# A two-layer graph network with residual and LayerNorm: splitting x from two buffers, zeroing only outer columns of the counts, four permits for counting, last two groups swapped

## The chip, the cores and the metric
One core of a Trainium2 chip runs the kernel. The metric is device microseconds of one execution. TensorE is called PE in the profile, VectorE DVE, ScalarE ACT, GpSimd POOL, SyncE SP.

## What is computed
The graph has N = 6250 nodes with D = 256 features and E = 100000 edges, sorted by destination; low nodes have the most edges. The reference is

```python
def agg(h, eps):                       # src, dst: (E,)
    return (1.0 + eps) * h + segment_sum(h[src], dst, N)
h = agg(x, eps1)                       # N x 256
h = relu(h @ W1a + b1a)                # 256 -> 512
h = relu(h @ W1b + b1b)                # 512 -> 512
h = agg(h, eps2)                       # N x 512
h = relu(h @ W2a + b2a)                # 512 -> 512
out = layernorm(x + h @ W2b + b2b)     # 512 -> 256, then over the features
```

## The kernel before
Nodes lie in NT = 49 tiles of 128 rows (the last has 106), edges in 782 chunks of 128. There are two ways to sum over edges.

**Light nodes: gathers.** For nodes above the first ten tiles (first eight in layer 2), GpSimd gathers the 128 source rows of a chunk with an indirect DMA (`gather`, L496), four chunks to a piece, six pieces of buffer. TensorE sums them with a matrix that selects slots (`sums`, L1180, L1211). Chunks form 78 groups, of which layer 1 takes the last 75 from the top down (`order`). `merge` (L1230) splits each sum in two parts on ScalarE and VectorE, moves it to node rows with two more matmuls (L1256) and adds it to the accumulators `acc` (L1268). When all groups that reach a tile are in, `dense` (L1289) runs the two matrix products of the layer on a block of one or two tiles (L1334, L1383, L1412) and stores the rows. The `acc` of layer 1 start as rows of x (`seeding`), scaled on ScalarE (`scaling`, L1081).

**Heavy nodes: counts.** For the ten lowest tiles, a matrix of edge counts from source to destination is built and multiplied with all of x. The 340 lowest chunks are counted in 245 steps, from high to low: 31 steps of one chunk in a window of W = 11 destination columns (two banks each), 149 steps of one chunk and width 7 to 10, 65 steps of two to eight chunks. A step (`counting`, L1851) makes two one-hot matrices on VectorE (`ca` L1883, `cb` L1893), multiplies them (L1936) into a bank, and then `counted_` (L1957) copies w - 1 columns of the window from the bank into the counts `at` or `at_first` with ScalarE (L1977) and adds the window's top column there with VectorE (L1985); the place comes from a register. So each copy overwrites columns and the top column is added to what the step before it wrote. Before, both count buffers are zeroed whole on ScalarE (`zeroing`, L1900; eight copies), and no step writes until that is done. A step takes a permit (`permits`, SIDE = 3) and returns it after its add; one-chunk steps of width 10 or less ask for two permits together:

```python
n = max(2 // (STEPS[i][1] * len(parts_of(STEPS[i][2]))), 1)
for _ in some:
    held_.append((yield ("get", permits, 0)))
```

In layer 1, `first_products` (L1668) multiplies the counts with x in three passes (tiles 9 and 8, then 7 to 4, then 3 to 0; L1811). A pass starts when the steps down to its lowest tile are done. For pass 0, `splitting` (L1677) loads four tiles of x into one buffer `raw`, cuts two tiles at a time into an upper and a lower part (two ScalarE copies L1696 and L1697, one VectorE subtraction L1699), and `storing` writes them to `halves` in HBM; `loading` reads them back for passes 1 and 2 once the last store is done. The count matrices are saved to HBM as well (L1783). In layer 2, `second_products` (L1528) multiplies them with h1 in 13 ranges of four tiles (the last, range 12, has one tile), from range 12 down to 0: counts are cast on ScalarE (`converting`, L1575), multiplied (L1648), and each product is added to `acc` (`taking`, L1586 and L1591). The rows of the first SOONER = 2 ranges are loaded and halved before layer 1 ends (`sooner`, L1762).

**Order of the work.** Preparation (up to the branch) turns the edge lists, builds tables and compares the data with the kernel's assumed bounds on VectorE (`violated`, L721); the sum of the violations is reduced at L834 and decides between `ordered` (this kernel) and a slow `general` branch. In `ordered` no engine order is dynamic: while the program is built, a class `Plan` (L296) plays all processes with estimated costs; engines, banks and buffers go to the process with the lowest number first, and the order in which it grants them is the order of each engine's instructions. Counting and sums ask for TensorE with 0, products of layer 1 with 1, dense work with 2, products of layer 2 with 3; SyncE's loads are issued where the plan reaches them. Each engine then runs its list in order and waits where a real time is later than the planned one. `filling` (L1275) puts dummy matmuls (L1280) into planned gaps late in layer 1 and at the start and in the second half of layer 2.

## Time and profile before

| | |
|---|---|
| median of 3 runs | 1537.58 us (1535.27 to 1547.84) |
| the profiled execution | 1526.32 us, of which the span is 1524.6 us |
| PE (matmul) busy | 1297.8 us, 85% of the span |
| DVE, ACT, POOL busy | 811.6 us (53%), 618.4 us (41%), 895.2 us (59%) |
| granted TensorE clock, mean | 0.935 |
| DMA | 304.29 MB, 200 GB/s in the mean |

The profile belongs to one execution; a row gives a line of the kernel, an engine, an operation, and what it writes and reads. An idle time is charged to the instruction after it and to what released that instruction; "issue" means that the view shows nothing it waited for, "remote" that it waited for something the view does not name. A granted clock of 0.50 is 1.2 GHz, 1.00 is 2.4 GHz.

### The profile page before, as it was taken

The numbers are of one execution on the slowest core, as the hardware profiler recorded it, in microseconds if no ns is written. First come the engines' busy times: TensorE is split into PE (matmuls) and PEld (weight loads), VectorE is DVE, ScalarE is ACT, GpSimd is POOL, SyncE is SP. The second block draws the span as 40 slices with busy tenths as digits, with TensorE's granted clock in tenths as the row PEclk, the third lists the DMA queues.
The fourth block names the chain that finished last, engine by engine and source line by source line (L and its number), as shares of the span: only waits on it lengthen the run. The fifth ranks groups of instructions, "written<-read, shape, count | busy, mean of one in ns | idle before, by whom it ended". The sixth has DMA issues, their size and how long they took to land.

```text
span 1524.6 us, 20531 instructions
## 1 busy us (share of the span) xinstructions
PE 1297.8 (85%) x6367; PEld 820.3 (54%) x6367; DVE 811.6 (53%) x2122; ACT 618.4 (41%) x1293; POOL 895.2 (59%) x944
## 2 busy tenths in 40 slices
PE   3478978879888899889968999997989999979997
PEld 2135545436554445555545666665556665656665
DVE  5575756655567883113146665764455544534343
ACT  3656556545555434444533423323233323321211
POOL 7565665565666766661256656664666666656640
PEclk7589988989999999999989999999999999999999
DMA  4555666647774436893478767776677877767650
GB/s 122 163 168 177 221 210 201 204 126 228 235 229 127 119 117 197 272 288 106 160 253 303 228 199 255 225 217 213 210 238 245 259 235 234 221 178 210 199 163 27
DMA packets 154445, 304.29 MB, mean 200 GB/s; under 512 B 34606, under 2 KB 69254, under 8 KB 154328
## 3 DMA queue, kind: packets, MB, share of 16 engines
q0 software_dynamic: 59136, 182.25, 39.6%
q1 hardware_dynamic: 87716, 107.04, 21.6%
q10 hardware_dynamic: 7476, 13.60, 2.5%
q8 instruction: 54, 0.88, 0.2%
q14 instruction: 63, 0.52, 0.1%
HBM read 263.18 MB, written 39.63 MB: 199 GB/s over the span
## 4 chain that ended last, share of the span: by engine, by line
PE 69%; DVE 9%; issue 8%; another core or an unknown queue 4%; ACT 4%; DMA 2%; POOL 1%; DVEq 1%; ACTq 1%; SPq 0%; POOLq 0%
PE bank L1383 17%; PE bank L1412 15%; PE bank L1211 11%; PE bank L1648 9%; PE bank L1811 7%; PE bank L1936 4%; PE bank L1256 4%; PE bank L1334 2%; DVE at L1985 1%; DVE cb L1893 1%; DVE acc L1591 1%; DVE acc L1268 1%; DMA xh<-halves 1%; DVE sel L1160 1%
## 5 line engine op out<-in xcount | busy, mean ns | idle before, releaser
L504 POOL DMA_INDIRECT early<-in_x_dram,srcs x442 | 435.9, 986 | 256.4 <-issue 113.0
L504 POOL DMA_INDIRECT early<-h,srcs x238 | 229.7, 965 | 186.5 <-issue 61.5
L504 POOL DMA_INDIRECT late<-h,srcs x236 | 227.2, 963 | 139.8 <-issue 59.1
L1268 DVE SCALAR_TENSOR_TENSOR acc<-bank,mask,acc 128x512 f32<-128x512 f32 (+1 forms) x365 | 210.9, 611 | 80.0 <-PE bank L1256 21.4
L1383 PE MATMUL bank<-zt,wide_w 128*128 128x256 f32 (+2 forms) x832 | 191.4, 387 | 24.5 <-ACT zt L1355 15.3
L1412 PE MATMUL bank<-wide_w,ht 128*128 128x512 f32 (+1 forms) x392 | 188.5, 607 | 3.2 <-DVE xh L1699 3.2
L1383 PEld LDWEIGHTS bank<-zt,wide_w 128*128 128x128 f32 x832 | 159.6, 203 | 55.6 <-ACT zt L1355 17.4
L1211 PE MATMUL bank<-early,sel 128*32 128x256 f32 (+1 forms) x1360 | 157.4, 489 | 30.2 <-issue 20.3
L1648 PE MATMUL bank<-upper,cfs 128*128 128x512 f32 (+1 forms) x392 | 169.4, 432 | 14.6 <-issue 10.9
L1811 PE MATMUL bank<-cf,xh 128*128 128x512 f32 (+2 forms) x588 | 150.2, 389 | 17.1 <-ACT cf L1752 10.2
L1648 PE MATMUL bank<-xr,cfs 128*128 128x512 f32 (+1 forms) x392 | 155.5, 397 | 0.0
L1977 ACT CAST at<-bank 128x250 f32 (+4 forms) x238 | 113.9, 494 | 99.7 <-PE bank L1936 32.6
L1575 ACT CAST cfs<-ci 128x512 fp32r<-128x512 uint8 (+3 forms) x104 | 60.7, 595 | 220.8 <-PE bank L1648 80.1
L1936 PE MATMUL bank<-cb,ca 128*128 128x490 f16 (+7 forms) x371 | 96.2, 340 | 58.6 <-DVE cb L1893 20.0
L1591 DVE TENSOR_TENSOR acc<-bank,acc 128x512 f32<-128x512 f32 x96 | 65.3, 684 | 137.9 <-remote 50.0
L1160 DVE TENSOR_TENSOR sel<-iota,slot 128x256 f32<-128x256 f32 (+3 forms) x109 | 47.6, 436 | 164.8 <-PE bank L1211 122.2
L1811 PEld LDWEIGHTS bank<-cf,xh 128*128 128x128 f32 (+1 forms) x588 | 100.8, 196 | 50.5 <-issue 20.7
L1256 PE MATMUL bank<-split,to 128*128 128x512 f32 (+3 forms) x306 | 89.8, 398 | 38.7 <-DVE split L1246 19.4
L1893 DVE TENSOR_SCALAR cb<-numbers,spot 128x492 f16<-128x492 f16 (+7 forms) x340 | 99.8, 330 | 40.0 <-remote 12.1
L1383 PE MATMUL bank<-zt,narrow_w 128*128 128x256 f32 (+2 forms) x432 | 103.3, 387 | 6.5 <-issue 4.0
L1211 PEld LDWEIGHTS bank<-early,sel 128*32 128x32 f32 x1360 | 40.0, 112 | 127.0 <-issue 107.0
L1412 PEld LDWEIGHTS bank<-wide_w,ht 128*128 128x128 f32 (+1 forms) x392 | 71.2, 193 | 66.7 <-issue 59.6
(150 smaller groups left out, 1702.4 us busy)
## 6 DMA issues: line engine op xcount, KB each, us to landing
xh<-halves SPq DMA_DIRECT2D x48, 512.0 KB
halves<-xh SPq DMA_DIRECT2D x24, 512.0 KB
h<-h1r ACTq DMA_DIRECT2D x48, 256.0 KB
xr<-h SPq DMA_DIRECT2D x12, 1024.0 KB
acc<-h SPq DMA_DIRECT2D x18, 512.0 KB
early<-in_x_dram,srcs POOLq DMA_INDIRECT x442
raw<-in_x_dram SPq DMA_DIRECT2D x12, 512.0 KB
r<-in_x_dram SPq DMA_DIRECT2D x22, 256.0 KB
```

The source lines that it names most:

```text
L504: nc.gpsimd.indirect_dma_start(out=rows_[:, j, :], out_offset=None, in_=table, in_offset=bass.IndirectOffsetOnAxis(ap=srcs[:, c : c + 1], ...
L1211: mm = nc.tensor.matmul(pm[b * SLOTS : (b + 1) * SLOTS], sel[:, c - groups[g][0], :], rows_[:, l, :], start=(c == part[0]), stop=(c == par ...
L1256: nc.tensor.matmul(pu[:, i * width : (i + 1) * width], to[:used], split[:used, l, i * width : (i + 1) * width], start=(l == 0), stop=(l == 1),
L1268: nc.vector.scalar_tensor_tensor(acc[t], pu[:, i * width : (i + 1) * width], mask[:, t - lo[g], g : g + 1], acc[t], op0=ALU.mult, op1=ALU.add,
L1383: nc.tensor.matmul(ph[:, (f - o) * TILES * P : (f - o) * TILES * P + nb], wa[:, k, f * P : (f + 1) * P], zt[:, k, :nb], start=(k == 0), st ...
L1412: nc.tensor.matmul(po[:m], ht[:, f, i * P : i * P + m], wb[:, f, :], start=(f == 0), stop=(f == KH - 1),)
L1591: nc.vector.tensor_tensor(acc[t], bank[token.number][:, :width], acc[t], op=ALU.add)
L1648: nc.tensor.matmul(bank[token.number][:, :width], cf[:m, j, :], of[:m, j, :], start=(j == 0 and of is upper), stop=(j == len(ks) - 1 and o ...
L1811: nc.tensor.matmul(to[:, :c], of, factor, start=(k == 0 and l == 0), stop=last, skip_group_check=True,)
L1893: made = nc.vector.tensor_scalar(token.tile[:, :e], numbers[:, :e], spot[:, c : c + 1], None, op0=ALU.is_equal,)
L1936: mm = nc.tensor.matmul(bank[token[l].number][:, : (k1 - k0) * w], a.tile[:, c % BATCH, :], b.tile[:, k0 * w : k1 * w], start=(j == 0), st ...
L1977: nc.scalar.copy(of[:, k0:k1, UNDER - w + 1 :][:, :, bass.ds(v, w - 1)], ap[:, :, : w - 1],)
```

## The change
- SIDE, the number of counting permits, goes from 3 to 4.
- `zeroing` writes, instead of all of `at`, only the columns from 976 on and those below 72 of its 1188, and all of `at_first`: three copies instead of eight. As the columns between are no longer zero, a step's top column must lie in the window that the step above it wrote. Preparation compares this for every step (`apart`), from a copy of the step's last nodes in SBUF (`before_`, ScalarE); the old compare of window widths stays for the first eight columns only.
- `splitting` has RAWS = 2 buffers of two tiles each; the planned wait before it goes from 60 to 50 (SPLIT), loads are issued as buffers come free, and a buffer is released once both ScalarE copies have read it. The scratch of the numbering moves to a tile of `ht_room`.
- In layer 1 the last two groups (4, then 3) change places. ENDING becomes a pair, 4 for layer 1 and 3 for layer 2.
- Layer 2 takes its ranges in the order 11, 10, ..., 0, 12, and `sooner` prepares ranges 11 and 10.

```diff
-SIDE = 3
+SIDE = 4
+SPLIT = 50.0
+RAWS = 2
-ENDING = 3
+ENDING = (4, 3)
+LAST = 0
...
+    def turn_order(number):
+        down = list(reversed(range(BEGIN[number - 1], NG)))
+        ending, down = down[:LAST], down[LAST:]
+        if number == 1:
+            down[-2:] = reversed(down[-2:])
+        return down + ending[::-1]
...
+        before_ = prep.tile([P, NC], F32, name="before_")
+        nc.scalar.copy(before_, cp)
         for k in range(halves):
             nc.scalar.copy(src_f[k], src_raw[k])
...
-        violated(compare, NC, near, wide_of, op=ALU.is_ge)
+        violated(compare, taken[0][2], near[:, : taken[0][2]], wide_of[:, : taken[0][2]], op=ALU.is_ge)
...
+        def apart(v):
+            for a, b, n, w in taken:
+                if a:
+                    add_compare(
+                        v[:, a - least_n : a - least_n + n], cp[:, a : a + n], -float(w),
+                        before_[:, a - 1 : a].to_broadcast([P, n]), op0=ALU.add, op1=ALU.is_ge,
+                    )
+                if b - a > n:
+                    add_compare(
+                        v[:, a + n - least_n : b - least_n], cp[:, a + n : b], -float(w),
+                        before_[:, a : b - n], op0=ALU.add, op1=ALU.is_ge,
+                    )
...
         violated(behind, NC - least_n)
+        violated(apart, NC - least_n)
...
+        range_order = [*reversed(range(len(ranges) - 1)), len(ranges) - 1]
...
-                raw_room = Tiles(loan, [P, RANGE, width], F32, "raw", 1)
-                scratch = raw_room.take()
+                raw_room = Tiles(loan, [P, PAIR, width], F32, "raw", RAWS)
+                scratch = ht_room.take()
...
-                rs = list(reversed(range(len(ranges))))
+                rs = range_order
...
                 def splitting():
-                    yield ("rest", 60.0)
-                    for r, ks in enumerate(ranges):
+                    yield ("rest", SPLIT)
+                    landed = []
+                    for q, ks in enumerate(spans):
                         raw = yield ("get", raw_room, 0)
                         in_rows(ks, raw.tile, table)
-                        yield ("rest", LOAD)
...
+                        landed.append(Event(plan))
+                        plan.at(plan.now + LOAD, landed[q].set)
+                        plan.start(parting(q, ks, raw, landed))
+
+                def parting(q, ks, raw, landed):
+                    yield ("until", landed[q])
+                    if q:
+                        yield ("until", parted[q - 1])
...
+                    nc.scalar.copy(xh[:m, :n, 0, :], of)
+                    nc.scalar.copy(ap, of)
+                    raw.release()
+                    parted[q].set()
...
-                    for i, r in enumerate(reversed(range(len(ranges) - SOONER, len(ranges)))):
+                    for i, r in enumerate(range_order[:SOONER]):
...
                 def zeroing():
-                    for k, (of, i, n) in enumerate(
-                        [(at, i, 7) for i in range(0, NT, 7)] + [(at_first, 0, NT)]
-                    ):
-                        some = of[:, i : i + n, :].rearrange("p a b -> p (a b)")
+                    over = (LOW[STEPS[0][0]] - BASE + UNDER) // 4 * 4
+                    under = -(-(HIGH[FINE] - BASE + UNDER + 1) // 4) * 4
+                    for some in (at[:, :, over:], at[:, :, :under], at_first):
                         some = some.bitcast(F32)
...
+                        nc.scalar.copy(
+                            some, zero.unsqueeze(2).to_broadcast(list(some.shape))
+                        )
```

## Rows read from the trace of the kernel before
**Rows 1.** The page, its first line.
```profile
span 1524.6 us, 20531 instructions
```
**Rows 2.** Windows by stage: stretch, length, busy time and count by engine, clock, DMA.
```profile
28.40:60.00 31.60, 10.31 (x52) 4.50 (x53) 15.78 (x49) 22.16 (x23) 21.50 (x22) 0.50 0.65 200
60.00:280.00 220.00, 176.62 (x897) 99.72 (x896) 145.99 (x403) 129.35 (x290) 132.34 (x136) 0.87 0.60 188
280.00:320.00 40.00, 26.53 (x124) 14.71 (x121) 25.74 (x71) 18.99 (x39) 19.93 (x22) 0.82 0.54 168
320.00:460.00 140.00, 124.22 (x631) 76.17 (x630) 79.66 (x224) 76.89 (x157) 88.07 (x91) 0.97 0.71 214
460.00:580.00 120.00, 105.21 (x534) 53.61 (x533) 94.97 (x308) 50.79 (x109) 79.77 (x79) 0.99 0.40 119
580.00:700.00 120.00, 109.13 (x543) 66.62 (x542) 25.71 (x55) 51.74 (x140) 76.48 (x80) 0.99 0.80 248
700.00:745.00 45.00, 44.66 (x206) 25.57 (x204) 11.44 (x21) 15.21 (x40) 0.00 (x0) 1.00 0.24 89
745.00:800.00 55.00, 38.99 (x155) 25.00 (x156) 18.79 (x33) 25.69 (x50) 31.96 (x33) 0.88 0.74 248
```
**Rows 3.** Timeline of VectorE in preparation: start, length, instruction, idle time before.
```profile
12.66 0.15 DVE L759 TENSOR_TENSOR viol<-cp,dstf 128x4 f16<-128x4 f32 x1
...
16.22 0.97 DVE L803 SCALAR_TENSOR_TENSOR viol<-heads,dstf 128x176 f16<-128x176 f32 x6
...
26.87 0.64 DVE L834 TENSOR_REDUCE fsum<-fp 1x1 f32<-1x473 f32 x1 [7.57 <-remote]
```
**Rows 4.** Timeline of TensorE and ScalarE, 40 to 60 us.
```profile
41.25 0.72 ACT L1081 ACTIVATE acc<-acc,e 128x512 f32<-128x512 f32 x1 [8.82 <-issue]
...
44.08 1.08 PE L1936 MATMUL bank<-cb,ca 128*128 128x275 f16 x4 [13.26 <-DVE cb L1893]
...
58.62 1.90 ACT L1977 CAST at<-bank 128x250 f32 x6
```
**Rows 5.** Groups on ScalarE, 40 to 60 us: busy, mean ns, idle before.
```profile
L1912 ACT COPY at<-zero 128x2079 f32<-128x2079 f32 x5 | 9.6, 1914 | 0.0
...
L1912 ACT COPY at_first<-zero 128x3381 f32<-128x3381 f32 x1 | 3.0, 3014 | 0.0
```
**Rows 6.** Groups on TensorE, 80 to 580 us, and on GpSimd, 60 to 580 us.
```profile
L1936 PE MATMUL bank<-cb,ca 128*128 128x490 f16 (+7 forms) x339 | 86.8, 333 | 39.0 <-issue 11.8 <-DVE cb L1893 6.8 <-DVE at L1985 6.4
...
L504 POOL DMA_INDIRECT early<-in_x_dram,srcs x325 | 320.8, 987 | 200.3 <-issue 82.3 <-PE bank L1211 45.8 <-PE bank L1936 41.4
```
**Rows 7.** Windows of the copy out of the bank (L1977, into at) alone.
```profile
80.00:120.00 40.00, 12.33 (x35) 0.83 0.53 170
...
200.00:240.00 40.00, 8.00 (x14) 0.88 0.65 205
...
560.00:600.00 40.00, 2.17 (x6) 1.00 0.53 155
```
**Rows 8.** The tile raw: ns min/median/max, first and last start in us.
```profile
L1696 ACT CAST xh<-raw x25: 395/619/641, 89.9 to 292.5; 128x512 fp32r<-128x512 f32 x24, 106x256 fp32r<-106x256 f32 x1
...
L867 SPq DMA_DIRECT2D raw<-in_x_dram x14: 338/373/535, 78.1 to 277.9; - x14
```
**Rows 9.** Timeline of TensorE and ScalarE at the change of layers.
```profile
746.24 0.50 PE L1648 MATMUL bank<-upper,cfs 106*128 106x512 f32 x1 [1.51 <-ACT cfs L1575]
...
753.44 0.40 PE L1648 MATMUL bank<-xr,cfs 106*128 106x512 f32 x1
...
754.37 0.39 PE L1648 MATMUL bank<-upper,cfs 128*128 128x512 f32 x1
754.60 0.39 PE L1648 MATMUL bank<-xr,cfs 128*128 128x512 f32 x1
...
775.33 0.62 ACT L1575 CAST cfs<-ci 128x512 fp32r<-128x512 uint8 x1 [12.04 <-remote]
...
776.00 0.80 PE L1648 MATMUL bank<-upper,cfs 128*128 128x512 f32 x1 [10.32 <-issue]
```

More of the change, by code (lines that the diff above doesn't have):

```diff
@@ L482, in tile_gin_residual_layernorm @@
         ]
+    def turn_order(number):
[4 more added lines that the diff above has]
+        return down + ending[::-1]
+    turns_of = {number: turn_order(number) for number in (1, 2)}
     pieces = {
@@ L486, in tile_gin_residual_layernorm @@
             (g, members[g][i : i + BURST])
-            for g in reversed(range(BEGIN[number - 1], NG)) for i in range(0, len(members[g]), BURST)
+            for g in turns_of[number] for i in range(0, len(members[g]), BURST)
         ]
@@ L939, in layer @@
             once = number == 1
-            order = list(reversed(range(BEGIN[number - 1], NG)))
+            order = turns_of[number]
             kk = width // P
@@ L983, in layer @@
             for t in reversed(range(NT)):
-                single = last_use.get(t, -1) >= len(order) - ENDING
+                single = last_use.get(t, -1) >= len(order) - ENDING[number - 1]
                 if taken and not single and len(taken) < TILES and (t >= tiles or (tiles - 1 - t) % TILES):
@@ L1145, in selecting @@
             def selecting():
-                for g in order:
+                for at_, g in enumerate(order):
                     if g in sels:
@@ L1150, in selecting @@
                     gs = [g]
-                    if h == 1 and g > order[-1] and groups[g - 1][1] == 1 and len(members[g - 1]) == PARTS:
+                    if (
+                        h == 1 and order[at_ + 1 : at_ + 2] == [g - 1] and groups[g - 1][1] == 1
+                        and len(members[g - 1]) == PARTS
+                    ):
                         gs.insert(0, g - 1)
@@ L1569, in converting @@
                 def converting(r, t, n, token, a):
-                    i = (len(ranges) - 1 - r) * tiles + t
+                    i = rs.index(r) * tiles + t
                     yield ("rest", LOAD)
@@ L1674, in first_products @@
                 stored = [Event(plan) for _ in spans]
+                parted = [Event(plan) for _ in spans]
                 factors = {}
                 def splitting():
[L1678 to L1679 removed]
+                    yield ("rest", SPLIT)
+                    landed = []
+                    for q, ks in enumerate(spans):
                         raw = yield ("get", raw_room, 0)
                         in_rows(ks, raw.tile, table)
[L1682 to L1706 removed]
@@ new lines, in splitting @@
+                        landed.append(Event(plan))
[5 more added lines that the diff above has]
+                        yield ("until", parted[q - 1])
+                    m, n = rows(ks[0]), len(ks)
+                    token = yield ("get", xh_room, 0)
+                    token.users = 2
+                    xh = token.tile
+                    of = raw.tile[:m, :n, :]
+                    bank_ = yield ("get", banks, 1)
+                    yield ("on", "ACT", 2 * act(n * width), 1)
+                    ap = bank[bank_.number][:m, : n * width].rearrange(
+                        "p (k d) -> p k d", d=width
+                    )
[3 more added lines that the diff above has]
+                    parted[q].set()
+                    yield ("on", "DVE", dve(n * width), 1)
+                    nc.vector.tensor_tensor(
+                        xh[:m, :n, 1, :], ap, xh[:m, :n, 0, :], op=ALU.subtract
+                    )
+                    bank_.release()
+                    xh_of[0, q] = token
+                    plan.then(halved[0, q].set)
+                    plan.then(plan.start, storing(q, token))
```

34 lines of the change are left out of this document (3 added, 31 removed).

## The prediction
> **What bounds the kernel now.** Read the page's span first [rows 1]: 1524.6 us, in an execution that took 1526.3 us, 11.3 us under the median of 1537.6 us of the runs shown. Then the windows by stage [rows 2], each of which has another limit. Preparation and the first stage of layer 1, up to 60 us, have TensorE at work for a third of the time or less: 10.3 of 31.6 us between 28.4 and 60, and at a granted clock of 0.50, the lower of its two levels (1.2 GHz). From 60 to 580 us TensorE works 80 to 89% of each stage, and no other engine does more; its idle time there adds up to 43.4 + 13.5 + 15.8 + 14.8 = 87.5 us. From 580 to 700 us it is at 91% with the DMA share at 0.80, from 700 to 745 us it is full (44.7 of 45). At the change of layers, 745 to 800 us, it loses 55.0 - 39.0 = 16.0 us. Behind that the change moves little. So the work of TensorE is fixed, and the question for each edit is which of its gaps closes.
>
> Three views say what makes those gaps. In the first stage, the timeline [rows 4] shows the first counting matmuls on TensorE at 44.08 us, but the first copy out of their banks on ScalarE only at 58.62 us. In between ScalarE works almost without a pause, and most of it is zeroing: of the seven copies into at, 1.914 us each, five lie there, and the one of 3.014 us into at_first [rows 5]. In the middle, the groups [rows 6] charge 39.0 us of TensorE's idle time between 80 and 580 us to the counting matmul (L1936), the largest share of any line, and GpSimd waits 41.4 us for that same line before it may start its next gathers. The rate of counting [rows 7] falls from 35 copies in 40 us to 14 after the one-chunk steps of width 10 and less begin, and counting ends only in the window 560 to 600; the last pass of products cannot start before. The splitting of x [rows 8] runs from 89.9 to 292.5 us, 25 pieces, 8.1 us each where the cast of a piece takes 0.62 us; the reloads for the later passes wait for its last store.
>
> **The change part by part.**
> *Preparation, +1 us.* The diff adds 32 compare instructions on VectorE. Nearest rows: a narrow compare takes 0.15 us, six compares of 176 columns take 0.97 us, so 0.16 us each [rows 3]. 32 x 0.16 = 5.2 us is the upper end. Behind them VectorE stands still for 7.57 us, until 26.87 us, before the reduction that decides the branch. No row names what it waits for. If that is an event of its own, the cost is 0; if it follows VectorE, 5.2. I take 1, near the lower end, because 7.57 covers 5.2. The added copy to before_ stands ahead of the conversion of the sources on ScalarE's queue and waits for the matmul of cp, so the sources and the gathers behind them come later too; that delay lies in the same 7.57. Were that cover gone, the sum would get 5.2 instead of 1. One further compare shrinks from 340 columns to 8, and one matmul is added: nothing, in the same cover.
>
> *Zeroing, -9 us.* The two rows of [rows 5] give (3014 - 1914) / (3381 - 2079) = 0.845 ns a column and 157 ns fixed. The three new copies have 49 x 53 = 2597, 49 x 18 = 882 and 3381 columns: 2.35 + 0.90 + 3.01 = 6.3 us against 16.4. They fit before 41.25 us, where ScalarE now stands idle for 8.82 us ahead of its first scaling [rows 4]; so what goes from the path is all zeroing after 41.25: five copies of 1.914 and the one of 3.014, 12.6 us. Next in line are the scalings between them and the splits of the first sums, which TensorE and GpSimd wait for as well, so gathers and counting both move forward. Bounds: 0 (the rows of acc land late and hold ScalarE anyway) and -12.6. I take -9, nearer the end that the continuous occupation of ScalarE supports.
>
> *Four permits instead of three, -6 us.* A step holds a permit from before its matmuls until VectorE has added its top column. The 149 one-chunk steps of width 10 and less ask for two permits at a time, so three permits let one pair run and four let two. Between 200 and 240 us there were 14 copies, that is 7 pairs, 5.7 us a pair, while ScalarE and VectorE work about 60% of that time [rows 2, 7]: the pairs wait for each other, not for an engine. Counting should end well before 560, and the last products with it. But TensorE had other work meanwhile; only its gaps count. Bounds: a third of the 87.5 us of idle time, -29, and +41.4, if more counting ahead of the sums doubles GpSimd's wait at that line. I take -6, less than a sixth of the 39.0 us charged to L1936, since TensorE is already near 85%.
>
> *Splitting from two buffers, begun 10 planned us earlier, -2 us.* The first load is issued at 78.1 and its rows are cast from 89.9 on [rows 8]: 11.8 us in which, with one buffer, no piece is ready. With two the load of one lies under the casts of the other. What is gained is a share of the 13.5 us that TensorE loses between 280 and 320, where pass 0 ends and pass 1 has no reloaded rows yet. Bounds 0 and -13.5; I take -2, because the counts of pass 1 are needed as well. The 12 further loads of SyncE's queue cost about 0.37 us each there [rows 8], 4.5 us over 200 us, ahead of halves stores and later seeds, which have time. The Trainium skill, DMA: Bandwidth & Descriptors, section "Anatomy of one DMA", gives each transfer a fixed cost of about 2.0 us, which speaks against two loads where there was one: an estimate of 24 us on the chain of loads, and if none of it overlapped this term would be 0 and the sum -21. No row here separates that fixed part.
>
> *Scratch of the numbering in ht's tile, selecting along the new order, ENDING (4, 3):* nothing. The last use of each tile gives the same blocks, and the first ht is wanted long after the numbering.
>
> *Last two groups of layer 1 swapped, 0.* Tile 8 is complete one group sooner. TensorE is full from 700 to 745 [rows 2], so the order of its last work shifts no end. Bounds +-2.
>
> *Ranges 11 and 10 ahead of layer 2 instead of 12 and 11, -7 us.* Range 12 has one tile: its 16 products stretch from 746.24 to 753.84 us [rows 9], 7.6 us, because each pair waits for a cast of its own on ScalarE. A matmul here follows the one before it after 0.23 us, so 16 are 3.7 us: 4 us of TensorE are lost, and with four-tile ranges a cast of 0.62 us serves eight matmuls. Then TensorE stands for 10.32 us until 776.00, behind ScalarE, which waits 12.04 us until 775.33 for something that the view does not name. With 64 products of range 10 at hand I count 3 of these 10 as filled. Bounds 0 and -16.0, the whole idle time of the window. The three more tiles to halve ahead (six copies of 512 columns, by the cast's 0.62 us some 3.7 us of ScalarE) lie in 700 to 745, where ScalarE works 15 of 45 us. Range 12 comes last now, with the same products as before.
>
> Sum: 1 - 9 - 6 - 2 + 0 - 7 = -23 us; 1526.3 becomes 1503, and the median 1537.6 becomes **1515 us**.
>
> **The rivals.**
> *Given back later (0.27), about 1532.* Layer 1 ends when the last sums and their dense work do, and TensorE is full there. If the gathers' chain gains nothing (it waits 45.8 us for the sums at L1211 and 41.4 at L1936 [rows 6], an order that the plan sets anew), the head start turns into more waiting before 580, and only the change of layers and a little of the start stay: -7 + 1 = -6. For it: 580 to 745 is nearly full. Against it: the gathers wait for TensorE, and TensorE's first sums wait for ScalarE.
> *Counting crowds out the sums (0.13), about 1561: slower.* Place: L1936 on TensorE's queue, ahead of L1211. With two pairs in flight GpSimd's 41.4 us behind L1936 double; +41.4 less the other terms (-9 - 2 - 7 + 1 = -17) is +24. It decides once the added wait passes 17 us. For it: the 31 steps of width 11 hold two banks each, and four of them hold all eight. Against it: banks come free earlier too, and 6.4 and 6.8 us of L1936's idle time are waits for the step before [rows 6].
> *The middle closes (0.12), about 1492.* Counting ends 80 us sooner, the last pass spreads over 460 to 580, where the DMA share is 0.40, and a third of the 87.5 us goes: -29 - 9 - 7 + 0 = -45.
> *The stricter compare sends the kernel down its general branch (under 0.01).* From the reference's destination list, every step's last node leaves at least two columns to the step below; the branch stays.
>
> **How the numbers follow.** The forecast has 0.48 and, with its terms' bounds, its own range 1500 to 1527. The range over the cases reaches from just below the closed middle (1490) to 1545, where some of the crowded case is left out. A measurement of this kernel can tell about 1%, 15 us, from no change. Faster by more: 0.8 of the forecast's 0.48, and the closed middle's 0.12: 0.50. Within: the rest of the forecast and nearly all that is given back: 0.36. Slower: 0.14.
>
> **What would show it.** Start: the first L1977 near 46 to 50 us instead of 58.6, and L834 still near 27. Counting: more than 16 copies in each window between 120 and 280, its end before 540. Splitting: done before 250 us. Change of layers: no products of 106 rows at its head, TensorE's idle time under 10 us. Wrong it would be if layer 1 still ends near 745 us, if L1936's idle time or GpSimd's wait there grows, or if layer 2 takes longer than the 779 us from 745 to the end.

## The result and the profile after

The changed kernel took 1549.5 us (median of 15 runs) against 1530.8 us for the kernel before beside it: ratio **1.0129, interval 1.0103 to 1.0155**, slower by 1.3%. The forecast was 1515 us, faster; the time also lies just above the range, which ended at 1545.

The times came at two levels, the same for all kernels of one series: the kernel before took about 1531 us in the first measurement and in the second and third series, and about 1286 us in the first, fourth and fifth; the chip does not decide it, since one chip showed both levels. I call them **with stops** and **without stops**, for waits that the traces show further down. The prediction was made on a trace with stops.

The profiled execution of the changed kernel spans 1554.6 us, 30.0 more than [rows 1]. Its windows by stage, columns as in [rows 2]:

```profile
28.40:60.00 31.60, 10.85 (x48) 4.19 (x47) 20.77 (x83) 15.86 (x31) 7.92 (x9) 1.00 0.56 160
60.00:280.00 220.00, 169.53 (x877) 96.60 (x877) 150.16 (x413) 133.05 (x294) 135.24 (x139) 0.94 0.62 197
280.00:320.00 40.00, 33.78 (x156) 18.12 (x154) 31.03 (x91) 23.35 (x47) 24.67 (x26) 0.91 0.44 133
460.00:580.00 120.00, 109.27 (x550) 60.52 (x552) 74.48 (x233) 47.56 (x114) 76.97 (x77) 0.96 0.48 144
700.00:745.00 45.00, 43.39 (x223) 24.58 (x222) 11.07 (x22) 15.53 (x39) 7.56 (x8) 1.00 0.35 118
745.00:800.00 55.00, 40.38 (x157) 25.85 (x156) 11.25 (x22) 24.08 (x41) 24.55 (x26) 0.84 0.58 181
```

Against [rows 2] TensorE gains 7 us in 280 to 320 and 4 in 460 to 580, and loses 7 in 60 to 280. GpSimd, 21.50 us busy from 28.4 to 60 in before, is busy 7.92 us there. Layer 1 starts late because its flag is late, as the timeline of VectorE shows (start, length, instruction, idle before; the stretch between the first two rows and the third is filled with rows like them, some of them 1.4 us apart):

```profile
13.94 0.17 DVE L792 SCALAR_TENSOR_TENSOR viol<-cp,before__331 128x8 f16<-128x8 f32 x1 [0.84 <-issue]
14.66 0.16 DVE L787 SCALAR_TENSOR_TENSOR viol<-cp,before__331 128x4 f16<-128x4 f32 x1 [0.43 <-issue]
...
36.48 0.16 DVE L828 TENSOR_TENSOR viol<-heads,dstf 128x2 f16<-128x2 f32 x1 [0.52 <-issue]
36.55 0.96 DVE L832 SCALAR_TENSOR_TENSOR viol<-heads,dstf 128x176 f16<-128x176 f32 x6
...
40.70 0.63 DVE L863 TENSOR_REDUCE fsum<-fp 1x1 f32<-1x473 f32 x1
```

Compares of 0.16 us start 0.7 us apart, from 13.9 to 36.5 us, and "issue" names no cause; then six take 0.96 us together. The reduction of [rows 3] comes at 40.70 instead of 26.87. ScalarE behind it, in order:

```profile
42.53 3.21 ACT L1947 COPY at<-zero 128x2597 f32<-128x2597 f32 x2
45.75 0.72 ACT L1111 ACTIVATE acc<-acc,e 128x512 f32<-128x512 f32 x1
46.38 2.99 ACT L1947 COPY at_first<-zero 128x3381 f32<-128x3381 f32 x1
49.28 1.94 ACT L1111 ACTIVATE acc<-acc,e 128x512 f32<-128x512 f32 x3
51.13 1.19 ACT L2014 CAST at<-bank 128x250 f32 x4
```

The zeroing takes 6.2 us, where 6.3 were foreseen, and the first copy out of the banks comes at 51.13, not 58.62 as in [rows 4], though its start was 14 us later. Counting and splitting also ended sooner, the last store of halves at 246.2 us. Yet layer 1 ends later. The last store of h1, first in the kernel before, then in the changed one (count, ns min/median/max, first and last start):

```profile
L867 ACTq DMA_DIRECT2D h<-h1r x50: 326/326/631, 95.6 to 745.5; - x50
```

```profile
L896 ACTq DMA_DIRECT2D h<-h1r x50: 326/326/605, 120.0 to 752.0; - x50
```

In these two traces 6.5 us are lost up to there, and layer 2 takes 1554.6 - 752.0 = 802.6 us against 1524.6 - 745.5 = 779.1: another 23.5. GpSimd's row of [rows 6], 60 to 580 us, reads in the changed kernel

```profile
L516 POOL DMA_INDIRECT early<-in_x_dram,srcs x326 | 321.0, 985 | 199.9 <-issue 81.8 <-PE bank L1244 61.8 <-PE bank L1973 34.6
```

The wait for the sums (L1244, before L1211) grew from 45.8 to 61.8 us, more than the wait for counting (L1973, before L1936) fell, 41.4 to 34.6. At the change of layers the 106-row products are gone, but TensorE still stops behind ScalarE's casts:

```profile
773.18 0.80 PE L1681 MATMUL bank<-upper,cfs 128*128 128x512 f32 x1 [3.47 <-ACT cfs L1608]
...
786.50 0.79 PE L1681 MATMUL bank<-upper,cfs 128*128 128x512 f32 x1 [9.10 <-ACT cfs L1608]
```

### The profile page after: what moved, and what is told of

Read it like the earlier page. It is cut to its first block, busy times and chain, and to the rows that moved or that the text cites. A ratio compares the mean times of both kernels' runs of the same rounds, so it can differ in the third digit from the quotient of the medians.

```text
span 1554.6 us, 20495 instructions
## 1 busy us (share of the span) xinstructions
PE 1311.2 (84%) x6357; PEld 818.6 (53%) x6357; DVE 815.1 (52%) x2154; ACT 608.7 (39%) x1289; POOL 887.0 (57%) x944
## 4 chain that ended last, share of the span: by engine, by line
PE 64%; DVE 13%; another core or an unknown queue 9%; issue 8%; ACT 3%; DVEq 1%; DMA 0%; POOL 0%; ACTq 0%
PE bank L1416 15%; PE bank L1445 14%; PE bank L1244 11%; PE bank L1681 8%; PE bank L1851 7%; PE bank L1973 4%; PE bank L1289 4%; DVE acc L1301 2%; PE bank L1367 2%; DVE acc L1624 1%; DVE at L2022 1%; DVE cb L1933 1%; ACT at L2014 1%; DVE split L1279 1%
## 5 line engine op out<-in xcount | busy, mean ns | idle before, releaser
L516 POOL DMA_INDIRECT early<-in_x_dram,srcs x442 | 431.3, 976 | 276.6 <-issue 112.3
L1445 PE MATMUL bank<-wide_w,ht 128*128 128x512 f32 (+1 forms) x392 | 193.4, 621 | 1.0 <-issue 1.0
L1244 PE MATMUL bank<-early,sel 128*32 128x256 f32 (+1 forms) x1360 | 164.3, 497 | 31.7 <-issue 13.2
L1681 PE MATMUL bank<-upper,cfs 128*128 128x512 f32 (+1 forms) x392 | 169.8, 433 | 16.7 <-ACT cfs L1608 14.6
L1851 PE MATMUL bank<-cf,xh 128*128 128x512 f32 (+2 forms) x588 | 152.7, 392 | 14.5 <-issue 8.9
L1973 PE MATMUL bank<-cb,ca 128*128 128x490 f16 (+7 forms) x371 | 99.5, 346 | 53.5 <-issue 18.6
L1289 PE MATMUL bank<-split,to 128*128 128x512 f32 (+3 forms) x306 | 86.3, 391 | 35.6 <-DVE split L1279 13.9
L1244 PEld LDWEIGHTS bank<-early,sel 128*32 128x32 f32 x1360 | 38.9, 113 | 136.1 <-issue 108.1
L1426 ACT ACTIVATE ht<-bank,b2a_s 128x256 f32<-128x256 f32 (+2 forms) x104 | 43.9, 458 | 157.7 <-PE bank L1416 56.1
```

Source lines behind the costliest of these rows:

```text
L516: nc.gpsimd.indirect_dma_start(out=rows_[:, j, :], out_offset=None, in_=table, in_offset=bass.IndirectOffsetOnAxis(ap=srcs[:, c : c + 1], ...
L1244: mm = nc.tensor.matmul(pm[b * SLOTS : (b + 1) * SLOTS], sel[:, c - groups[g][0], :], rows_[:, l, :], start=(c == part[0]), stop=(c == par ...
L1289: nc.tensor.matmul(pu[:, i * width : (i + 1) * width], to[:used], split[:used, l, i * width : (i + 1) * width], start=(l == 0), stop=(l == 1),
L1445: nc.tensor.matmul(po[:m], ht[:, f, i * P : i * P + m], wb[:, f, :], start=(f == 0), stop=(f == KH - 1),)
L1681: nc.tensor.matmul(bank[token.number][:, :width], cf[:m, j, :], of[:m, j, :], start=(j == 0 and of is upper), stop=(j == len(ks) - 1 and o ...
L1851: nc.tensor.matmul(to[:, :c], of, factor, start=(k == 0 and l == 0), stop=last, skip_group_check=True,)
```

## The experiments

In the diffs a line of the changed kernel (or of the kernel before, where that is said) is marked -, and ... stands for lines left out. All ratios are to the kernel before in the same series.

**First series, without stops (before 1287.2 us): parts of the change undone.**

a1_no_apart: without the new compares.

```diff
-        nc.scalar.copy(before_, cp)
...
-        violated(compare, taken[0][2], near[:, : taken[0][2]], wide_of[:, : taken[0][2]], op=ALU.is_ge)
+        violated(compare, NC, near, wide_of, op=ALU.is_ge)
...
-        violated(apart, NC - least_n)
```

> The changed kernel without the 32 new compares and without before_ (the compare of near against wide_of is the old one over 340 columns); this leaves out the test that the narrower zeroing needs. Everything behind the branch is the changed kernel's. Theory (the added instructions of VectorE fall into a stretch in which each costs 0.7 to 1.4 us, and the flag that decides the branch comes 13.8 us later for them): the flag's cast falls back from 41.4 to about 27 to 29 us, and the kernel gets 11 to 14 us shorter than the changed one, ratio to the kernel before about 1.004. Rival (the slow stretch is there in any case, and the flag waits for GpSimd's gathers that the later sources delay): the cast stays above 36 us and the time within 4 us of the changed kernel's, ratio about 1.011 to 1.013.

a2_old_ranges: the old order of ranges; a5_no_apart_old_ranges: both diffs together.

```diff
-        range_order = [*reversed(range(len(ranges) - 1)), len(ranges) - 1]
+        range_order = list(reversed(range(len(ranges))))
```

> The changed kernel with the old order of ranges in layer 2 (12, 11, ... 0). Theory (the new order costs layer 2 some 20 us: 802.6 us against 779.1 from the last write of h1 to the end): layer 2 takes 776 to 785 us, the flag's cast stays near 41 us, and the kernel is 18 to 24 us shorter than the changed one, ratio to the kernel before 0.998 to 1.001. Rival (layer 2's loss is a matter of where its instruction stalls fall, not of the order): layer 2 stays over 795 us, ratio 1.008 or more.

> Both of these undone together: the narrower zeroing (without the test that it needs), the two buffers, four permits and the swap stay. Theory: the gains add, 11 to 14 and 18 to 24 us less than the changed kernel, ratio to the kernel before 0.988 to 0.994, so faster than both. Rival (the later start of layer 1 is filled by other work, or layer 2 has its loss from elsewhere): ratio 1.000 or more.

a4_side3: three permits.

```diff
-SIDE = 4
+SIDE = 3
```

> The changed kernel with three permits for counting, as before. Theory (four permits shorten layer 1 a little, by the 6 us that the prediction gave them or less): 0 to 8 us longer than the changed kernel, ratio 1.013 to 1.018; counting ends later than in the changed kernel. Rival (the fourth permit crowds out the sums and costs time): shorter than the changed kernel by 5 us or more, ratio under 1.010, and GpSimd's waits for L1244 fall back from 64.0 and 69.6 us.

Measured: a1 **0.9994** (0.9972 to 1.0016), a2 **1.0072** (1.0049 to 1.0096), a5 **1.0051** (1.0023 to 1.0079), a4 **0.9942** (0.9920 to 0.9963). Both theories on the order fell here: with the old order the kernel is slower, a5 against a1 by 0.57%. Three permits do more than all else: a4, whose rival's numbers came, is the only one that is faster than the kernel before. a1 met neither of its cases, since its ratio lies below both. The compares cost 0.2% (a2 against a5), less than the two intervals can tell apart. The flag shows their cost directly, first a1, then a4 (cast of the flag: ns, first and last start):

```profile
L847 DVE CAST flag<-fsum x1: 141/141/141, 19.0 to 19.0; 1x1 int32<-1x1 f32 x1
```

```profile
L864 DVE CAST flag<-fsum x1: 141/141/141, 20.3 to 20.3; 1x1 int32<-1x1 f32 x1
```

The new test puts the flag off by 1.3 us, not 13.8.

**Second series, with stops (before 1531.2 us).** after_again and before_again are the two kernels unaltered.

> The changed kernel itself, unaltered, beside its variants. Where the kernel before takes about 1287 us, as in the last four runs, and not 1531: theory (the loss of 1.3% came from stalls of all engines that these runs lack): a ratio between 0.999 and 1.004, which would follow from the variant without the compares (0.9994) and the cost of 32 compares at 0.16 us. Rival (the loss is the same whatever the stalls): 1.010 to 1.016, as first measured. Where the kernel before takes about 1531 us again: 1.010 to 1.016 by both.

> The kernel before, unaltered, for its trace. Ratio 1. Theory (what made 1531 us of 1287 is that engines now and then get no instructions for 4 to 12 us or get them at 0.7 or 1.4 us each): where it takes 1287 us, the 7.6 us stop of VectorE ahead of the flag, the 13.3 us of TensorE at 44 us and the 12.0 us of ScalarE at 775 us are gone or under 3 us each, and the matmuls take as long as before one by one. Rival (a slower chip: all durations longer): the same stops stand in the trace, and single instructions are 15% shorter.

after_again: **1.0089** (1.0056 to 1.0122). before_again is a single execution of 1540.5 us, and shows what one profile is worth here. Its timeline of VectorE ahead of the flag:

```profile
18.96 0.97 DVE L799 TENSOR_TENSOR viol<-heads,dstf 128x176 f16<-128x176 f32 x6 [5.96 <-remote]
...
30.20 0.57 DVE L818 CAST slot<-sloti 128x784 f16<-128x784 int32 x1 [6.45 <-remote]
...
36.65 0.64 DVE L834 TENSOR_REDUCE fsum<-fp 1x1 f32<-1x473 f32 x1 [4.10 <-remote]
```

The same instructions as in [rows 3], the reduction 9.8 us later: of the 13.8 us that the first two traces seemed to show, 9.8 are within what one kernel does from run to run. Waits in all of this trace that no engine and no transfer ends (us in total, times, longest):

```profile
ACT cfs L1575 <- remote: 79.6, 11, 9.9
DVE acc L1591 <- remote: 63.0, 14, 9.9
ACT ht L1393 <- remote: 26.3, 7, 7.9
POOL early L504 <- remote: 23.8, 12, 2.8
```

No trace without stops has a row that ends "remote". Single instructions are not shorter there: the sum into acc takes 611 ns in the profile of before and 612 in that of the changed kernel without stops (after_fourth below), a gather 986 and 985, a product 432 and 435. What differs first is this standing still, of ScalarE, VectorE and GpSimd. TensorE's busy time differs too: of the 267.4 us between the profile of the changed kernel here (1554.6) and in after_fourth (1287.2), 99.3 are busy time of TensorE (1311.2 and 1211.9 us, at a mean granted clock of 0.951 and 0.967). What causes the stops, no run here shows.

a7_compact_side3: three permits, and the test with fewer instructions.

```diff
-SIDE = 4
+SIDE = 3
...
-        nc.scalar.copy(before_, cp)
...
-            for a, b, n, w in taken:
+            for a, b, n in counted_spans:
...
-                    add_compare(
-                        v[:, a + n - least_n : b - least_n], cp[:, a + n : b], -float(w),
-                        before_[:, a : b - n], op0=ALU.add, op1=ALU.is_ge,
+                    compare(
+                        v[:, a + n - least_n : b - least_n], nearer[:, a + n : b],
+                        cp[:, a : b - n], op=ALU.is_ge,
...
+        nc.vector.tensor_tensor(nearer, cp, wide_of, op=ALU.subtract)
```

> The changed kernel with three permits and with the new test in fewer instructions: the widths subtracted from cp once, then one or two compares for each span of equal count instead of one or two for each step, and without before_. Theory: 2 to 3 us less than the changed kernel with three permits (0.9942) where instructions come at full pace, so 0.990 to 0.993 and faster than both kernels; 8 to 14 us less where they come at 0.7 us. Rival (VectorE's preparation has cover): the same as three permits alone, 0.994.

b1_before_new_ranges: the kernel before with the new order alone.

```diff
+        range_order = [*reversed(range(len(ranges) - 1)), len(ranges) - 1]
...
-                rs = list(reversed(range(len(ranges))))
+                rs = range_order
...
-                    i = (len(ranges) - 1 - r) * tiles + t
+                    i = rs.index(r) * tiles + t
...
-                    for i, r in enumerate(reversed(range(len(ranges) - SOONER, len(ranges)))):
+                    for i, r in enumerate(range_order[:SOONER]):
```

> The kernel before with the new order of ranges in layer 2 alone (11, 10, ... 0, 12). Where the kernel before takes about 1287 us: theory (the order gains where engines get their instructions in time: 0.57% between the two variants without the compares): 4 to 9 us shorter, ratio 0.993 to 0.997. Rival (the order only gains together with the rest): within 2 us, 0.998 to 1.002. Where the kernel before takes about 1531 us: 10 to 24 us longer by the first reading of the two traces, ratio 1.006 to 1.015.

a7 **1.0046** (1.0014 to 1.0077): lower than the changed kernel's 1.0089, though the intervals overlap, and not better than the kernel before, against both its cases. b1 **1.0046** (1.0002 to 1.0089): with stops the order loses. One execution of b1 took 6732.1 us; it is not in the ratio, and no trace of it was kept. The median of all twelve, 1543.1 us, is 0.8% above the kernel before.

**Third series, with stops (before 1527.4 us): parts alone.** c1_before_side4 is the kernel before with `SIDE = 4`; d1_zeroing_splitting_swap is the diffs of a1, a2 and a4 together; the other two are repeats.

> The kernel before with four permits for counting instead of three, and nothing else. Theory (the fourth permit makes counting crowd out the sums of layer 1; three permits instead of four took layer 1 of the changed kernel from 623 to 614 us where no engine stands still for an unseen reason): 6 to 11 us longer than the kernel before, ratio 1.004 to 1.008, on either sort of chip; GpSimd's waits for the sums' line grow. Rival (the prediction's term): 0 to 8 us shorter, ratio 0.995 to 1.000.

> The changed kernel without three of its parts: three permits, the old order of ranges, and no new compares (the test that the narrower zeroing needs is left out). What is left of the change is zeroing of outer columns, splitting from two buffers, the swap and ENDING. Theory (these parts bring the gain that the prediction gave them): 4 to 12 us shorter than the kernel before, ratio 0.992 to 0.997 on either sort of chip. Rival (they gain nothing by themselves, since layer 1's end is set by TensorE): within 2 us, 0.998 to 1.002.

> The changed kernel itself once more. Theory: where the kernel before takes about 1287 us, a ratio between 0.998 and 1.004, the fourth permit's 9 us against the new order's 7 and the zeroing's; where it takes about 1531 us, between 1.007 and 1.014 as the two times before. Rival (the ratio has nothing to do with the engines' unseen stops): 1.009 to 1.013 in both cases.

> The kernel before with the new order of ranges alone, once more. Theory: where the kernel before takes about 1287 us, 6 to 13 us shorter, ratio 0.990 to 0.996, all of it in layer 2; where it takes about 1531 us, 1 to 13 us longer again, ratio 1.001 to 1.009. Rival (the order alone does the same on every chip): the same sign in both cases.

c1 **1.0151** (1.0085 to 1.0217), d1 **0.9958** (0.9923 to 0.9994), after_third **1.0117** (1.0081 to 1.0152), b1_again **1.0083** (1.0042 to 1.0125). The zeroing, the two buffers and the swap gain together about 6 us; the fourth permit alone loses about 23 (interval 13 to 33), more than the 6 to 11 that were expected of it, and the order alone loses 7 and 13. In c1 the windows by stage are

```profile
60.00:280.00 220.00, 158.06 (x778) 87.10 (x778) 143.59 (x403) 120.45 (x265) 124.10 (x129) 0.82 0.52 160
...
700.00:745.00 45.00, 44.60 (x204) 22.83 (x202) 12.09 (x25) 13.02 (x29) 21.02 (x22) 1.00 0.39 121
```

18.6 us of TensorE are lost between 60 and 280 against [rows 2], and GpSimd still gathers for layer 1 in the stretch where before it had finished (21.02 us busy against 0.00). The last store of h1 is at 776.5 us.

**Fourth series, without stops (before 1286.4 us).** c3_before_late_fourth, from the kernel before: the fourth permit only once the steps with two banks have asked.

```diff
-SIDE = 3
+SIDE = 4
...
+                spare = yield ("get", permits, 0)
                 i = 0
                 while i < len(STEPS):
+                    if spare and len(parts_of(STEPS[i][2])) == 1:
+                        spare.release()
+                        spare = None
```

> The kernel before with a fourth permit that is given only once the steps of width 11, which hold two banks each, have all asked. Theory (four such steps hold all eight banks, so sums, products and splitting find none early in layer 1, which is where four permits from the start cost 1.5%): the cost is gone, ratio 0.995 to 1.003, the splitting ends near 296 us as before, not near 342. Rival (two pairs of narrow steps in flight crowd out the sums throughout): 1.008 or more.

e1_before_twelve_third is b1's diff with another list; f1_best is the diffs of a2 and a7 together; f2_best_twelve_third is a7 with the order of e1.

```diff
+        range_order = [len(ranges) - 2, len(ranges) - 3, len(ranges) - 1, *reversed(range(len(ranges) - 3))]
```

> The kernel before with the ranges in layer 2 in the order 11, 10, 12, 9, 8, ... 0: the new order's head, the old order's end. Theory (the new order costs time at its end: TensorE has its products done about 50 us sooner and nothing to fill the stops of the last 150 us): the cost is gone, ratio 0.994 to 1.002. Rival (it costs at its head, where two ranges of four tiles are loaded and halved while layer 1 ends): 1.004 to 1.010 as for the whole new order. Where the kernel before takes about 1287 us, theory 0.990 to 0.996.

> The changed kernel with three permits, the old order of ranges, and its test in fewer instructions (widths subtracted from cp once, a compare or two for each span of equal count). Nothing is left out. Theory: as the same kernel without the test (0.9958), so 0.993 to 1.000, and faster than the changed kernel by 1 to 2%. Rival (the test's instructions cost as much as the prediction's upper end or more): 1.002 or more.

> The kernel of the run before this one (three permits, the test in fewer instructions) with the ranges in the order 11, 10, 12, 9, ... 0. Theory (the new order's head gains, its end loses): 2 to 8 us shorter than with the old order, ratio 0.989 to 0.996. Rival (the head loses): 5 to 13 us longer than with the old order.

c3 **1.0103** (1.0077 to 1.0129): the theory that four steps of two banks fill all eight fell, since a fourth permit costs 13 us without any step of two banks. e1 has layer 1 of the kernel before but for two early loads at its end, so its trace beside c3's shows the cost. GpSimd's waits for TensorE, 120 to 400 us, first e1, then c3:

```profile
POOL early L504 <- PE bank L1937: 3.5, 11, 0.4
```

```profile
POOL early L504 <- PE bank L1936: 13.3, 16, 3.7
POOL early L504 <- PE bank L1211: 10.7, 10, 4.1
```

24.0 us behind counting (L1936, in e1 L1937) and the sums (L1211), against 3.5 behind counting; e1's list has no wait for the sums in this stretch. And the windows, first e1, then c3:

```profile
120.00:280.00 160.00, 149.99 (x826) 88.92 (x825) 125.86 (x330) 110.39 (x228) 122.20 (x125) 0.99 0.79 248
400.00:580.00 180.00, 173.64 (x910) 103.49 (x909) 92.70 (x278) 86.49 (x213) 132.08 (x135) 1.00 0.72 226
580.00:630.00 50.00, 49.94 (x225) 27.64 (x223) 12.96 (x23) 18.67 (x45) 0.00 (x0) 1.00 0.26 88
```

```profile
120.00:280.00 160.00, 140.71 (x758) 78.74 (x757) 133.33 (x358) 112.81 (x237) 117.32 (x120) 0.97 0.71 226
400.00:580.00 180.00, 179.74 (x909) 107.84 (x907) 74.45 (x201) 83.34 (x204) 136.39 (x138) 1.00 0.73 225
580.00:630.00 50.00, 50.00 (x245) 28.46 (x244) 11.75 (x23) 15.65 (x38) 10.59 (x11) 1.00 0.33 101
```

With four permits VectorE and ScalarE do more early (the counting), TensorE 9.3 us less; from 400 on TensorE is full, and eleven gathers are left over for the end. Counting was sooner and the layer later.

TensorE's own waits say where the cost arises. In c3, 60 to 400 us, they have among them dense work (L1412, L1383) and sums (L1211) behind counting's add:

```profile
PE bank L1412 <- DVE at L1989: 5.5, 3, 3.2
PE bank L1211 <- DVE at L1989: 4.5, 3, 2.0
...
PE bank L1383 <- DVE at L1989: 2.0, 2, 1.2
```

These matmuls do not read `at`; what they share with a counting step is the pool of eight banks, and a step gives its bank back after that add. Waits of this kind (matmuls other than counting's, behind counting's copy or add, from 60 to 470 us, with stops to 560) add up to 0.3 to 1.9 us in the five traces without stops that have three permits and to 5.4 to 14.5 in the five with four; with stops to 1.0 to 6.0 in six traces with three and to 17.6 to 31.7 in four with four. So the rows point to banks after all, held by steps of one bank too; a run that changes the banks alone was not made.

e1 **0.9947** (0.9927 to 0.9967), f1 **1.0011** (0.9991 to 1.0031), f2 **0.9955** (0.9936 to 0.9974). The order with range 12 third gains as the whole new order does. f1 came out just above its theory: zeroing, splitting and swap, worth 6 us with stops, show no gain without (its short test put the flag at 19.2 us, against 19.0 with the old one).

**Fifth series, without stops (before 1285.0 us).**

> The kernel with three permits, the test in fewer instructions and the order 11, 10, 12, 9, ... 0 once more. Where the kernel before takes about 1531 us: theory (the new order loses at its end, for lack of products there) ratio 0.988 to 0.998; rival (it loses at its head) 1.001 to 1.008, as the same kernel with the whole new order (1.0046). Where it takes about 1287 us: 0.9955 again, within 0.993 to 0.998.

> The changed kernel once more. Where the kernel before takes about 1287 us: theory (fourth permit +0.5%, new order -0.6%, the new test +0.2%, the rest nothing) 0.999 to 1.004; rival (1.3% slower everywhere) 1.009 or more. Where it takes about 1531 us: 1.007 to 1.014 as three times before.

f2_again **0.9946** (0.9921 to 0.9972), so faster than both kernels; after_fourth **1.0015** (0.9994 to 1.0036): the changed kernel is no slower here than the kernel before, as the sum of its parts said. The slowdown of 1.3% belongs to the level with stops, but what does the damage in layer 1 is there at both.

The length of each layer, from the flag's cast to the last store of h1, and from there to the span's end, makes the terms plain. Without stops, layer 1 takes 610.5 to 613.8 us in the five traces with three permits (a4, e1, f1, f2 twice) and 622.9 to 625.3 in the five with four (a1, a2, a5, c3, after_fourth): **in the mean 11.6 us for the fourth permit**. Layer 2 takes 652.4 to 655.2 us in the old order (a2, a5, c3, f1) and 641.4 to 645.7 in the new (a1, a4, after_fourth): **10 us gained by the order**. With stops layer 2 takes 779.1 to 789.6 us in the old (before, before_again, c1, d1) and 787.9 to 802.6 in the new (b1 twice, a7, the changed kernel three times): **13 us lost in the mean**, 8 in b1's two traces alone, and the two ranges touch.

Layer 1 with stops is less plain: 706.6 to 723.1 us in the six traces with three permits, 708.8 to 713.1 in the three of the changed kernel, 756.0 in c1. A late flag can shorten this length, since part of the delay is made up: in before_again, with its flag 9.8 us later than in before, the last store of h1 came only 3.7 us later. On the clock, the means of the changed kernel's three traces lie 19.5 us above those of the two of the kernel before: 3.8 us of that up to the last store of h1, 15.7 behind it. So most of the measured loss lies in layer 2.

## Why the prediction was wrong

*Preparation (+1).* The size was right without stops (1.3 us). With stops the cover named, the 7.57 us ahead of the reduction, was one of those stops and no event of its own: it is absent without them, and in another trace of the same kernel stops of 6.0, 6.5 and 4.1 us stood there. The upper end, 5.2, assumed that instructions come at their own pace; they came at 0.7 us. With the new compares the flag was cast at 38.2 to 41.4 us in three traces, in the kernels with the old test at 20.5 to 37.3 in six. The short test of a7 had it at 38.8, so it is open how much of this the number of instructions makes.

*Zeroing (-9), splitting (-2).* The mechanism held: without stops the first copy moves from 41.0 (e1) to 31.0 us (after_fourth). But the 10 us do not reach the end there: layer 1 takes 613.0 us in f1 and 611.9 in e1. That is the first rival's course, given back later: TensorE is full at the end of the layer. With stops the two gained, with the swap, 6 us (interval 1 to 12) instead of 11.

*Four permits (-6).* This is one of the two steps that failed: the term counted TensorE's gaps as room to be filled and put no price on the banks that the steps in flight hold. I read 14 copies in 40 us [rows 7] as pairs that wait for each other at a cost, and took counting's end for what the last pass waits for. Counting did end at 545 us instead of 579, near what I foresaw, and no gain came of it: alone the permit costs 23 us with stops (c1) and 13 without (c3). Early on counting did not even speed up: from 120 to 240 us the changed kernel makes 44 copies, as many as before. It was the second rival, to which I gave 0.13, but not by its way: the cost without stops is 11.6 us instead of 41.4, and by the waits in c3 it arises where dense work and sums wait for a bank, which in turn holds up the gathers behind the sums (without stops, from 60 to 470 us GpSimd waits 0.9 to 2.2 us at the sums with three permits and 10.7 to 19.8 with four). With stops GpSimd's wait at the sums is no clean sign: it grew from 45.8 to 61.8 us here, but b1, with three permits and the old layer 1, has 55.4 and 57.4 from 60 to 560 us. The rival's argument with steps of two banks is not the cause (c3), and mine that banks come free earlier did not save the term.

*Ranges (-7).* At the level at which the prediction was made this is the other step that failed, and the larger part of the loss: the order alone costs 7 and 13 us (b1 twice). Without stops it gained 10 us, the size foreseen, but by luck. The term counted the products of 106 rows, each pair behind its own cast, and a stop at the head; TensorE's waits for the casts in the first 160 us of layer 2 are 2.8 us in a2, in the old order, and 2.0 in after_fourth. What the new order removed is a stop 75 us into the layer, of the matmul that moves sums to node rows, behind VectorE's split of them; in a2 it reads

```profile
718.96 2.50 PE L1289 MATMUL bank<-split,to 128*128 128x512 f32 x5 [9.38 <-DVE split L1279]
```

The longest wait of this kind is 8.1 to 10.4 us in the four traces with the old order; in after_fourth all of them in these 160 us are 0.6. With stops the prediction took 3 of the 10.32 us of TensorE's stand at 776.00 [rows 9] as work to be filled; that stand came from ScalarE's "remote" wait of 12.04, and the changed kernel has such waits of 6.6, 12.2 and 10.7 us between 765 and 813 us. Where the loss lies, the last 150 us of each execution show, first before, then the changed kernel:

```profile
1374.60:1524.60 150.00, 131.92 (x674) 95.42 (x673) 56.75 (x138) 28.12 (x67) 65.09 (x68) 0.93 0.50 149
1404.60:1554.60 150.00, 122.72 (x627) 84.78 (x626) 48.96 (x120) 27.39 (x67) 55.86 (x59) 0.92 0.44 132
```

TensorE stands still there for 17.9 to 18.7 us in the four traces with stops in the old order and for 24.4 to 29.4 in the six in the new: about 9 of the 13 us. The last product of the ranges starts 51 to 53 us before the end in the old order and 97 to 103 in the new, so TensorE has less to do while the others stop. That this is the reason is argued, not shown: the order with range 12 third, which ends as the old one does, was only run without stops. ScalarE's "remote" waits behind layer 1 point the same way, 111 to 135 us in those four traces and 117 to 170 in the six, but overlap.

*Swap and scratch (0).* Not taken apart; they lie within d1.

*The sum.* With stops the chain before, d1, a7, changed kernel reads -6 us (zeroing, splitting, swap), +13 (order, short test), +10 (fourth permit, long test), from ratios 0.9958, 1.0046 and the mean 1.0112 of three; each step is good to some 5 us, and the first joins two series. The permit's 10 us in this chain stand beside 23 in c1; why it costs less in the changed kernel is open. The edits that gained at their place were outweighed by two others: one that holds banks which the sums and dense work need, and one that leaves TensorE idle at the end. One reading was off as well: from 280 to 320 us TensorE works 26.5 of 40 us [rows 2], which is 66% and not 80 to 89%; the splitting's term used the right 13.5 us. Of the signs that I had named as proof of error, two came, layer 1 past 745 and layer 2 past 779; the third named counting's line, where TensorE's idle time (39.0 and 37.9 us) and GpSimd's wait fell. Of the good signs the splitting's end before 250 and a head without products of 106 rows came; counting's end missed 540 by 5 us, only one of the four windows from 120 to 280 had more than 16 copies (16, 12, 16, 24), the first copy came at 51.1 and the reduction at 40.7, and the change of layers kept 55.0 - 40.4 = 14.6 us of idle TensorE where I had said under 10.

*Two loads for one.* The prediction named a price for a transfer's fixed part from the Trainium skill, DMA: Bandwidth & Descriptors, "Anatomy of one DMA". That section describes transfers that GpSimd issues, and the loads here are SyncE's, so no run here tests its figure. No loss showed: from the first load to the last store of halves the splitting took 53.9 to 246.2 us instead of 78.1 to 295.9, with 26 loads for 14.

## What to carry to other kernels

Side work that may run further ahead also holds more of what it shares with the main work, here banks: the main work's waits for it grew from under 2 us to 5 and more, though the side work ended up to 34 us sooner. Look for such waits before giving side work more room. Before a gap is counted as something to fill or as cover, look at what ended it: a gap ended by "remote" moves from run to run, and needs a second trace of the same kernel. Judge parts alone or taken out one at a time; here a sum near nothing (1.0015) held +12 and -10 us.

## What the runs showed of the hardware

The same program takes 1286 or 1531 us, 19% more. Single instructions of VectorE and GpSimd take the same time at both levels; with stops, engines stand without a named reason or start instructions of 0.16 us at a distance of 0.7 us, and TensorE's busy time is 99 us longer in two traces of one kernel. The Trainium skill, Runtime: NRT & Kernel Launch, "Instruction fetch mechanics", describes engines whose instructions are refilled from memory in blocks, and calls the cost of crossing a block's edge mostly hidden; no run here shows whether the stops have to do with that. An edit's sign can depend on this level: the order of ranges gained 0.6% without stops and lost 0.5 to 0.8% with them.
